# Graph-attention layers on Trainium2: target scores as three bfloat16 numbers, spread by a bfloat16 zero-one matrix

## The chip, the core and the metric

The kernel runs on one core of a Trainium2 chip. The core has five instruction streams: TensorE (PE in the profile, its weight loads PEld), VectorE (DVE), ScalarE (ACT), GpSimd (POOL) and SyncE (SP, which here only starts transfers). The metric is the device time of one run in microseconds. Three runs of the kernel before gave a median of 2871.9 us (2867.6 to 2875.4).

## The reference

The input is `x` of 8 batches x 2048 nodes x 128 features and one symmetric adjacency matrix with about 17 neighbours per node. Four layers follow one another: attention, graph, attention, graph. The change touches the two graph layers only, numbered 1 and 3. Such a layer computes

```python
h = x @ W
s_i = h @ a_src
s_j = h @ a_dst
e = s_i[:, :, None] + s_j[:, None, :]
e = jnp.where(e >= 0, e, NEG_SLOPE * e)
e = jnp.where(adj[None, :, :] == 0, -jnp.inf, e)
att = jax.nn.softmax(e, axis=-1)
out = jnp.einsum('bij,bjd->bid', att, h)
y = out + x
```

and then a layer norm. `s_i` is the score of the target node, the one that receives; `s_j` that of the source, its neighbour.

## The kernel before

**Sparse tiling.** The 2048 nodes are cut into 32 units of 64 target nodes. The neighbours of a unit's targets are listed in up to 9 tiles of 128 slots, one slot being one edge; they are handled as `TG = 5` steps `t`, four of two tiles each and a last one of a single tile. On the 128 partitions of a gathered tile lie 128 edges. The four batches of each half of the batch (`HB = 4`, two halves) lie beside each other, so a slot has 2 x 4 scores.

**Rows.** Each layer leaves a table in DRAM with one row per node: for a graph layer the source score, the 128 features and a one per batch. An indirect transfer that GpSimd starts (`gather`, L1711) fetches the 128 rows of a tile. Its buffers are six `kv` rings, and each ring is shared by four tiles in a graph layer.

**Targets.** A target's score is made a layer earlier, when that layer's result is projected (`project`): `spread_out` (L1613) writes it into the constant tile `self.t[:, u]`, 128 partitions x 16 columns. The partitions are the targets of the two halves in groups of 32, the 16 columns are 4 groups x 4 batches, and all but the own group is zero.

**The zero-one matrices.** Tile `hot` (float32, 960 columns) has two parts. Columns 0 to 639 say for each target which slots are its own (`fetch`): ScalarE writes the distance of the slot number from the middle of a target's slots (L1439), VectorE compares it with half the length (L1446). Columns 640 to 959 say for each slot which target it has (`slots`, L1357, called at L1464). For the first four units (`LATE = 4`) a second piece is added (L1457 to L1461).

**A unit of a graph layer.** `opened_graph` spreads the target scores over the slots: one matmul per step `t` with 128 columns of `hot` as the stationary operand and `self.t` as the moving one, into the PSUM tile `ps_te` (L2091). VectorE takes a large number from the scores of empty slots and writes `te` (`mask`, L2106 to L2115). Then, for each step, in `graph`: VectorE adds target and source score and applies the slope (`score`, L2030 and L2037), ScalarE takes the exponential (L2042), VectorE multiplies the exponentials by the zero-one matrix, giving `w` (`fold`, L2052), and PE multiplies `w` with the gathered rows and adds up in PSUM (`add`, L2068: 16 matmuls for a step of two tiles, 8 for the last). After five steps `after_graph` divides, adds the residual, norms, and projects to the next layer's table (layer 1) or writes the output (layer 3).

**The order of the work.** No loop order is written down for the engines. Each operation is given to a planner (`Plan`) with its estimated cost per engine, a key (layer x 1000 + unit x 5 + step, less or plus an offset) and the tiles it reads and writes. The planner plays the run through with these costs and takes on each engine the ready operation of lowest key; an operation is only taken when its buffers are free. The order that comes out is fixed into the program, each engine then runs its list strictly in order, and waits are semaphores. So a changed cost or a new operation can shift the order of everything that the planner decides later. Operations marked `port=True` are kept by the planner from running on VectorE and GpSimd at once; a gather (`port="wait"`) isn't started while one runs. Work with a lowered key is prepared ahead: the score matmuls have key base - 3, the building of `hot` base - 8, gathers key - 12.

Of the kernel before, what the change touches and what calls it, by code (L numbers as in the profile page):

```python
# [11 lines left out]
BF16 = mybir.dt.bfloat16  # L12
F16 = mybir.dt.float16
F8 = mybir.dt.float8e5
I32 = mybir.dt.int32
AF = mybir.ActivationFunctionType
ALU = mybir.AluOpType
# [3 lines left out]
P = 128  # L21
# [11 lines left out]
GROUP = 32  # L33
UNIT = 2 * GROUP
TG = 5
TILES = 2 * TG - 1
GS = TG * P
# [3 lines left out]
HOT = GS + 2 * TG * GROUP  # L41
# [8 lines left out]

SBUF_BUFS = {
    "kv": 6, "hot": 3, "hot8": 5, "x": 4, "q_sb": 2, "rows": 3, "at": 1, "r": 2, "x1": 2, "hidden": 1, "normed": 2,
    "xnew": 2, "trows": 2, "s": 2, "ex": 7, "var": 2, "rstd": 2, "rc": 2, "te": 2, "e": 4, "w": 3,
    "cand": 2, "aux": 3, "aux16": 3, "unit_aux": 2, "some": 2, "rank_e": 2, "pick": 1,
    "gap": 1, "late": 1,
}
# [544 lines left out]
class Plan:  # L601
# [35 lines left out]
    def cell(self, tag, shape, dtype=F32, name=None):  # L637
        pool = self.pools[tag]
        return Cell(tag, lambda: pool.tile(shape, dtype, name=name or tag, tag=tag))

    def op(self, costs, fn, key, reads=(), writes=(), joins=(), holds=(), shares=(), port=False, dma=0):


        o = Op({e: us * self.share for e, us in costs.items()}, fn, key, port, dma)
        shares = [*shares, *(c.whole for c in (*reads, *writes, *joins, *holds) if c.whole)]
        before = set()
        for c in reads:
            before.update(c.writers)
        for c in writes:
            before.update(c.writers)  # L650
            before.update(c.readers)
        for c in joins:
            before.update(c.readers)
        for c in reads:
            c.readers.append(o)
        for c in writes:
            c.writers, c.readers = [o], []
        for c in joins:
            c.writers.append(o)
        before.update(w for c in holds for w in [c.owner, *c.writers] if w)  # L660
        for c in dict.fromkeys([*writes, *joins, *reads, *holds, *shares]):
            if c.tag:
                if not c.owner:
                    c.owner = o
                    o.allocs.append(c)
                c.left += 1
                o.cells.append(c)
        for b in before:
            b.next.append(o)
        o.waits = len(before)  # L670
        o.behind = [c.owner for c in (*shares, *joins) if c.tag and c.owner is not o]
        self.ops.append(o)
# [130 lines left out]
class Sparse:  # L803
# [602 lines left out]
    def fetch(self, n, u, key):  # L1406

        x = self.cell("x", [P, CH])
        self.op(
            {"SP": 0.45},  # L1410
            lambda e: e.dma_start(out=x.tile, in_=self.xd[u] if n else self.xt_in[u]),
            key,
            reads=[self.x_at[u] if n else self.gates[20]],
            writes=[x],
            dma=P * CH * 4,
        )
        hot = self.cell("hot", [P, HOT])
        if n == 0 and u < KEPT:
            hot8 = self.kept[u]
            self.op({"ACT": 1.05}, lambda e: e.copy(hot.tile, hot8.tile), key - 15, reads=[hot8], writes=[hot])  # L1420
            return x, hot
        if LAYERS[n] is MHA:
            hot8 = self.cell("hot8", [P, HOT], F8)
            self.op(
                {"SP": 0.45},
                lambda e: e.dma_start(out=hot8.tile, in_=self.hots[u]),
                key,
                reads=[self.hots_at[u]],
                writes=[hot8],
                holds=[hot],  # L1430
                dma=P * HOT,
            )
            self.op({"ACT": 1.05}, lambda e: e.copy(hot.tile, hot8.tile), key + 4, reads=[hot8], writes=[hot])
            return x, hot

        ends, oht = self.ends[:, u, :], lambda: hot.tile[:, 0:GS]
        self.op(
            {"ACT": 0.82},
            lambda e: e.activation(oht(), self.slot, AF.Abs, bias=ends[:, 0:1]),  # L1439
            key + 4,  # L1440
            reads=[self.ends_at[u]],
            writes=[hot],
        )
        self.op(
            {"DVE": 0.4},
            lambda e: e.tensor_scalar(oht(), oht(), ends[:, 1:2], None, ALU.is_le),  # L1446
            key + 4,
            writes=[hot],
            port=True,
        )  # L1450
        if u < LATE:
            after = self.cell("late", [P, P])
            self.op(
                {"ACT": 0.3}, lambda e: self.late_targets(e, after.tile, u), key + 4, reads=[self.ends_at[u]], writes=[after], holds=[hot]
            )

            def both(e):  # L1457
                shared = hot.tile[:, GS - P : GS]
                e.scalar_tensor_tensor(shared, after.tile, self.late_ends[:, u, 1:2], shared, ALU.is_le, ALU.add)

            self.op({"DVE": 0.25}, both, key + 4, reads=[after], writes=[hot])  # L1461
        self.op(
            {"DVE": 0.5},
            lambda e: self.slots(e, hot.tile, self.owner[:, u]),  # L1464
            key + 4,
            reads=[self.idx_at[u]],
            writes=[hot],
            port=True,
        )
        return x, hot  # L1470

    def whole(self):

# [517 lines left out]
    def graph(self, n):  # L1991
        hb = self.HB
        width = hb * (P + 2)
        op, cell = self.op, self.cell
        made = {}
        for u, i in self.sequence(LATE):
            base = n * STRIDE + u * TG
            if not i:
                made[u] = self.opened_graph(n, u, base)
            x, hot, te, outs, banks = made[u]  # L2000
# [5 lines left out]
            if u < LATE:  # L2006
                t, at = i, u * 2 * PAIRS + 2 * i if i < PAIRS else LATE * 2 * PAIRS + u
                key = base + i if i < PAIRS else n * STRIDE + LATE * TG - 2 + u / LATE
            else:
                t = i if u % 2 == 0 else (i - 1) % TG  # L2010
# [35 lines left out]
            w = cell("w", [P, 2 * hb, 2, GROUP])  # L2046

            def fold(e, t=t, hot=hot, e8=e8, w=w, tiles=tiles):
                oh = hot.tile[:, GS + 2 * t * GROUP : GS + (2 * t + 2) * GROUP].rearrange("p (j c) -> p j c", j=2)
                for j in range(0, 2, tiles):  # L2050
                    shape = [P, tiles, 2 * hb, GROUP]
                    e.tensor_tensor(  # L2052
                        w.tile[:, :, j : j + tiles, :].rearrange("p x j c -> p j x c"),
                        oh[:, j : j + tiles].unsqueeze(2).to_broadcast(shape),
                        e8.tile[:, 0:tiles].unsqueeze(3).to_broadcast(shape),
                        ALU.mult,
                    )
# [23 lines left out]
    def opened_graph(self, n, u, base):  # L2081
        hb = self.HB
        op, cell = self.op, self.cell
        x, hot = self.fetch(n, u, base - 12)

        ps = cell("m", [P, TG, 4 * hb], name="ps_te")
        te = cell("te", [P, TG, 2, 2, hb])

        def spread(e, u=u, ps=ps, hot=hot):
            for t in range(TG):  # L2090
                e.matmul(  # L2091
                    ps.tile[:, t, :],
                    lhsT=hot.tile[:, t * P : (t + 1) * P],
                    rhs=self.t[:, u, :],
                    start=True,
                    stop=True,
                )

        op({"PE": 0.8}, spread, base - 3, reads=[hot, self.t_at[u]], writes=[ps], holds=[te])

        def mask(e, u=u, ps=ps, te=te):
            last = TG - 1
            scores = ps.tile.rearrange("p t (h j b) -> p t h j b", h=2, j=2)
            empty = self.empty[:, u, 0 : 2 * last].rearrange("p (t j) -> p t j", j=2).unsqueeze(3)
            for hf in range(2):
                e.tensor_tensor(  # L2106
                    te.tile[:, 0:last, hf],
                    scores[:, 0:last, hf],
                    empty.to_broadcast([P, last, 2, hb]),
                    ALU.subtract,  # L2110
                )

            own = te.tile[:, last, :, 0, :]
            e.tensor_scalar(own, scores[:, last, :, 0, :], self.empty[:, u, 2 * last :], None, ALU.subtract)
            e.tensor_tensor(own, scores[:, last, :, 1, :], own, ALU.add)  # L2115

        op({"DVE": 0.6}, mask, base - 3, reads=[ps, self.idx_at[u]], writes=[te])

        if u % 2 == 0:
            outs = [cell("q", [P, 4, CH], name="acc_q")]  # L2120
            banks = [lambda outs=outs, k=k: outs[0].tile[:, k, :] for k in range(2)]
        else:
            outs = [cell("acc", [P, CH]), cell("m", [P, CH], name="acc_m")]
            banks = [lambda outs=outs, k=k: outs[k].tile for k in range(2)]
        return x, hot, te, outs, banks
# [165 lines left out]
```

## Time and profile before

| what | before |
|---|---|
| median of 3 runs | 2871.9 us |
| profiled execution, whole | 3119.97 us |
| its span, first to last instruction | 3118.2 us |
| mean granted TensorE clock | 0.883 |
| PE busy / instructions | 2427.8 us (78%) / 21668 |
| DVE busy / instructions | 2312.8 us (74%) / 3782 |
| ACT busy | 1432.0 us (46%) |
| POOL busy | 2126.9 us (68%) |
| bytes moved by DMA | 1022.48 MB, mean 328 GB/s |
| matmuls of the target scores | first 1137.8 us, last 3074.0 us |

The profile is one execution with the hardware profiler on, and it is 248 us longer than the median run; durations of single instructions come from it. Each row of its groups names a line and engine, the operation, the tiles written and read with their shapes, a count, the busy time and the mean of one in ns, and after the last bar how long the engine had been idle just before such instructions and what ended that. A float32 matmul leaves two matmul records and two weight-load records, a 16-bit one leaves one of each. "issue" is time in which an engine waited for nothing that the profile shows. "remote" or "an unknown queue" is a releaser that the trace can't name. The chain of waits goes back from the last instruction to what released it, step by step, so it shows what the end hung on.

The layers follow one another with some overlap; the two graph layers are seen at the score matmuls, from about 1140 to 1620 us and from about 2620 to 3100 us.

### The profile page before, as it was taken

To read this page: it belongs to the slowest core of one execution; us is meant where nothing else is said; L and a number is where in the kernel's file an instruction comes from. 1 tells how busy PE (TensorE), PEld (TensorE's weight loads), DVE (VectorE), ACT (ScalarE), POOL (GpSimd) and SP (SyncE) were. 2 spreads that over 40 slices of the span, in tenths; PEclk is the share of its full clock that TensorE was granted. 3 is DMA by queue.
4 is the path that set the end of the run, shared out by engine and by line. 5 is a ranking of instruction groups with operands and counts; after the bars stand their busy time and mean duration, and the time that the engine had idled before them with its cause. 6 is when DMAs were issued, how large, how long until landed. Compare 5 with 4: busy or idle time off the path is not lost.

```text
span 3118.2 us, 59203 instructions
## 1 busy us (share of the span) xinstructions
PE 2427.8 (78%) x21668; PEld 1343.1 (43%) x21668; DVE 2312.8 (74%) x3782; ACT 1432.0 (46%) x4900; POOL 2126.9 (68%) x1465
## 2 busy tenths in 40 slices
PE   6677877878888858877886888888888876777775
PEld 4423333333333346655664333333333335555554
DVE  8798988998999944444436889989899984555555
ACT  6455455555554425444443444445454432333332
POOL 1387877888888645555543888888888864655552
PEclk8788888899999978998877999999999987877787
DMA  7888889898899879999996899999999977999994
GB/s 301 331 328 304 315 312 345 325 355 334 345 382 357 314 255 332 353 353 338 334 320 244 344 363 376 367 379 375 369 358 373 379 264 242 341 314 315 315 312 157
DMA packets 248057, 1022.48 MB, mean 328 GB/s; under 512 B 39184, under 2 KB 52880, under 8 KB 175856
## 3 DMA queue, kind: packets, MB, share of 16 engines
q0 software_dynamic: 166464, 864.44, 74.0%
q1 hardware_dynamic: 81296, 154.18, 13.6%
q8 instruction: 174, 2.85, 0.4%
q14 instruction: 123, 1.01, 0.1%
HBM read 978.23 MB, written 88.08 MB: 342 GB/s over the span
## 4 chain that ended last, share of the span: by engine, by line
PE 33%; DVE 19%; issue 17%; POOL 12%; DMA 12%; ACT 4%; another core or an unknown queue 2%; POOLq 0%; SPq 0%; DVEq 0%; ACTq 0%
DMA kv<-table,idx 8%; POOL kv L1817 7%; DVE kv L1784 7%; POOL kv L1711 5%; PE acc_q L2068 5%; PE qe L1772 4%; PE acc L1869 4%; DVE s L1791 3%; PE ps_c L1535 3%; PE acc_m L2068 2%; PE ps_p L1573 2%; PE acc L2068 2%; PE ps_f L1545 2%; DMA hot<-hots 2%
## 5 line engine op out<-in xcount | busy, mean ns | idle before, releaser
L1711 POOL DMA_INDIRECT kv<-table,idx x1152 | 1189.4, 1032 | 756.9 <-issue 281.3
L1817 POOL TENSOR_TENSOR kv<-kv,ex 128x2048 f32<-128x2048 f32 x260 | 923.4, 3567 | 94.9 <-ACT ex L1801 90.6
L1784 DVE TENSOR_TENSOR kv<-qe,kv 128x2048 f32<-128x2048 f32 (+1 forms) x320 | 661.8, 2068 | 94.3 <-DMA kv<-table,idx 44.7
L1791 DVE TENSOR_REDUCE s<-kv 128x128 f32<-128x2048 f32 (+1 forms) x320 | 660.5, 2064 | 12.5
L1772 PE MATMUL qe<-q_sb,hot 32*128 32x512 f32 (+1 forms) x2304 | 393.4, 685 | 144.3 <-DVE kv L1784 134.6
L1869 PE MATMUL acc<-kv,hot 128*32 128x512 f32 (+1 forms) x2304 | 362.9, 640 | 54.1 <-POOL kv L1817 43.9
L2052 DVE TENSOR_TENSOR w<-hot,e 128x512 f32<-128x512 f32 (+1 forms) x384 | 222.4, 598 | 200.4 <-remote 64.6
L2068 PE MATMUL acc_q<-kv,w 128*32 128x129 f32 (+1 forms) x4608 | 255.5, 318 | 100.9 <-issue 69.0
L2068 PEld LDWEIGHTS acc_q<-kv,w 128*32 128x32 f32 (+1 forms) x4608 | 178.8, 130 | 168.7 <-issue 117.4
L1772 PEld LDWEIGHTS qe<-q_sb,hot 32*128 32x128 f32 (+1 forms) x2304 | 106.5, 194 | 333.6 <-DVE kv L1784 223.7
L1801 ACT ACTIVATE ex<-s 128x128 f32<-128x128 f32 (+1 forms) x320 | 95.3, 298 | 286.9 <-DVE s L1791 245.5
L1647 ACT ACTIVATE junk<-ps_c 128x128 f32<-128x128 f32 x492 | 136.0, 276 | 161.1 <-PE ps_c L1535 131.3
L2068 PE MATMUL acc<-kv,w 128*32 128x129 f32 (+1 forms) x2304 | 146.2, 321 | 67.6 <-issue 29.3
L2068 PE MATMUL acc_m<-kv,w 128*32 128x129 f32 (+1 forms) x2304 | 163.3, 315 | 42.7 <-issue 42.0
L1545 PE MATMUL ps_f<-x,W 128*128 128x512 f32 (+1 forms) x264 | 164.1, 715 | 39.8 <-ACT x L1690 18.3
L1511 ACT COPY trows<-ps_p 128x258 f32<-128x258 f32 (+1 forms) x237 | 112.4, 476 | 161.0 <-PE ps_p L1575 77.8
L1535 PEld LDWEIGHTS ps_c<-centre,r 128*128 128x128 f32 x1024 | 131.4, 200 | 107.4 <-DVE r L1941 56.7
L1535 PE MATMUL ps_c<-centre,r 128*128 128x128 f32 x1024 | 154.4, 296 | 26.0 <-DVE r L1941 21.0
L1961 ACT ACTIVATE hidden<-ps_f,b 128x512 f32<-128x512 f32 (+1 forms) x130 | 87.8, 676 | 154.9 <-PE ps_f L1545 136.8
L1680 ACT ACTIVATE normed<-ps_c,rstd 128x128 f32<-128x128 f32 x494 | 143.7, 368 | 9.6 <-issue 3.5
L1869 PEld LDWEIGHTS acc<-kv,hot 128*32 128x32 f32 (+1 forms) x2304 | 55.1, 114 | 213.7 <-issue 108.9
L1522 PE MATMUL ps_t<-ident,normed 128*128 128x128 f32 x638 | 119.8, 309 | 32.3 <-ACT xnew L1690 18.1
(204 smaller groups left out, 3761.0 us busy)
## 6 DMA issues: line engine op xcount, KB each, us to landing
x<-xd SPq DMA_DIRECT2D x96, 256.0 KB
xd<-xnew SPq DMA_DIRECT2D x93, 256.0 KB
kv<-table,idx POOLq DMA_INDIRECT x1152
table<-trows SPq DMA_DIRECT2D x128, 130.0 KB
kv<-adj_dram SPq DMA_DIRECT2D x16, 1024.0 KB
table<-trows SPq DMA_DIRECT2D x32, 512.0 KB
table<-trows SPq DMA_DIRECT2D x64, 256.0 KB
kv<-xk_dram SPq DMA_DIRECT2D x8, 1024.0 KB
```

Of the source, the lines that this page charges most:

```text
L1535: e.matmul(ps.tile[:, cols], lhsT=flat(x.tile)[:, cols], rhs=self.centre, start=True, stop=True)
L1545: lambda e: e.matmul(ps.tile, lhsT=w, rhs=x.tile, start=True, stop=True),
L1647: e.activation(self.junk, x, AF.Square, scale=P**-0.5, accum_out=var.tile[:, b, 1:2])
L1680: e.activation(out, in_, AF.Copy, scale=by)
L1711: e.indirect_dma_start(out=rows(kv.tile, j), out_offset=None, in_=self.tables[n][0:nodes], in_offset=bass.IndirectOffsetOnAxis(ap=self.idx ...
L1772: e.matmul(qe.tile[:, j, hf, :], lhsT=hot.tile[rows, t * P : (t + 1) * P], rhs=q.tile[rows, :], start=True, stop=True,)
L1784: e.tensor_tensor(k, qe.tile[:, 0:tiles].rearrange("p j h c -> p (j h) c"), k, ALU.mult)
L1791: e.tensor_reduce(s.tile[:, 0 : tiles * heads].rearrange("p (q c) -> p q c", q=2 * tiles), k, axis=mybir.AxisListType.X, op=ALU.add,)
L1817: e.tensor_tensor(v, v, w.unsqueeze(3).to_broadcast([P, 2 * tiles, heads // 2, HD]), ALU.mult)
L1869: e.matmul(out[rows, :], lhsT=hot.tile[:, col : col + GROUP * (3 - tiles)], rhs=rhs[:, 2 * j + hf, :], start=(t == 0), stop=(t == TG - 1),)
L2052: e.tensor_tensor(w.tile[:, :, j : j + tiles, :].rearrange("p x j c -> p j x c"), oh[:, j : j + tiles].unsqueeze(2).to_broadcast(shape), e ...
L2068: e.matmul(acc(b)[at : at + GROUP * (3 - tiles), :], lhsT=w.tile[:, hf * hb + b, j : j + 3 - tiles, :].rearrange("p j c -> p (j c)"), rhs= ...
```

## The change

The matrix `hot` of a graph layer is held as bfloat16 in the first half of the same tile, and the distances before the compare as float16 in the same place. The target scores of a unit are split on VectorE into three bfloat16 numbers each: the score rounded, the rest rounded, and the rest of that; the rests overwrite `self.t`. The three go side by side into one matmul per step with 48 columns in place of 16, all operands bfloat16, and VectorE adds the three in a reduction out of PSUM before it masks. The new tile `thirds` has two buffers. The weight product reads its zeros and ones from the bfloat16 matrix. The planner's cost of the score matmuls goes from 0.8 to 0.6, of the masking from 0.6 to 0.85, and the split is entered with 0.4. The attention layers are not edited.

```diff
-    "xnew": 2, "trows": 2, "s": 2, "ex": 7, "var": 2, "rstd": 2, "rc": 2, "te": 2, "e": 4, "w": 3,
+    "xnew": 2, "trows": 2, "s": 2, "ex": 7, "var": 2, "rstd": 2, "rc": 2, "te": 2, "thirds": 2, "e": 4, "w": 3,
...
-        ends, oht = self.ends[:, u, :], lambda: hot.tile[:, 0:GS]
+        ends = self.ends[:, u, :]
+
+        def numbers():
+            return hot.tile[:, 0 : HOT // 2].bitcast(F16)[:, 0:GS]
+
+        def low():
+            return self.low(hot)
+
...
-            lambda e: e.activation(oht(), self.slot, AF.Abs, bias=ends[:, 0:1]),
+            lambda e: e.activation(numbers(), self.slot, AF.Abs, bias=ends[:, 0:1]),
...
-            lambda e: e.tensor_scalar(oht(), oht(), ends[:, 1:2], None, ALU.is_le),
+            lambda e: e.tensor_scalar(low()[:, 0:GS], numbers(), ends[:, 1:2], None, ALU.is_le),
...
-                shared = hot.tile[:, GS - P : GS]
+                shared = low()[:, GS - P : GS]
...
-            lambda e: self.slots(e, hot.tile, self.owner[:, u]),
+            lambda e: self.slots(e, low(), self.owner[:, u]),
...
+    def low(self, hot):
+
+        return hot.tile[:, 0 : HOT // 2].bitcast(BF16)
...
-                oh = hot.tile[:, GS + 2 * t * GROUP : GS + (2 * t + 2) * GROUP].rearrange("p (j c) -> p j c", j=2)
+                oh = self.low(hot)[:, GS + 2 * t * GROUP : GS + (2 * t + 2) * GROUP].rearrange("p (j c) -> p j c", j=2)
...
-        ps = cell("m", [P, TG, 4 * hb], name="ps_te")
+        thirds = cell("thirds", [P, 3, 4 * hb], BF16)
+
+        def split(e, u=u, thirds=thirds):
+            rest = self.t[:, u, :]
+            for k in range(3):
+                e.tensor_copy(thirds.tile[:, k, :], rest)
+                if k < 2:
+                    e.tensor_tensor(rest, rest, thirds.tile[:, k, :], ALU.subtract)
+
+        op({"DVE": 0.4}, split, base - 5, writes=[self.t_at[u], thirds])
+        ps = cell("m", [P, TG, 3, 4 * hb], name="ps_te")
...
-                    ps.tile[:, t, :],
-                    lhsT=hot.tile[:, t * P : (t + 1) * P],
-                    rhs=self.t[:, u, :],
+                    ps.tile[:, t].rearrange("p k c -> p (k c)"),
+                    lhsT=self.low(hot)[:, t * P : (t + 1) * P],
+                    rhs=thirds.tile.rearrange("p k c -> p (k c)"),
...
-        op({"PE": 0.8}, spread, base - 3, reads=[hot, self.t_at[u]], writes=[ps], holds=[te])
+        op({"PE": 0.6}, spread, base - 3, reads=[hot, thirds], writes=[ps], holds=[te])
...
-            scores = ps.tile.rearrange("p t (h j b) -> p t h j b", h=2, j=2)
+            e.tensor_reduce(
+                te.tile.rearrange("p t h j b -> p t (h j b)"),
+                ps.tile.rearrange("p t k c -> p t c k"),
+                axis=mybir.AxisListType.X,
+                op=ALU.add,
+            )
+            scores = te.tile
...
-        op({"DVE": 0.6}, mask, base - 3, reads=[ps, self.idx_at[u]], writes=[te])
+        op({"DVE": 0.85}, mask, base - 3, reads=[ps, self.idx_at[u]], writes=[te])
```

More of the change, by code (lines that the diff above doesn't have):

```diff
@@ L2084, in opened_graph, with spread @@
         x, hot = self.fetch(n, u, base - 12)
-        ps = cell("m", [P, TG, 4 * hb], name="ps_te")
+        thirds = cell("thirds", [P, 3, 4 * hb], BF16)
[7 more added lines that the diff above has]
+        ps = cell("m", [P, TG, 3, 4 * hb], name="ps_te")
         te = cell("te", [P, TG, 2, 2, hb])
-        def spread(e, u=u, ps=ps, hot=hot):
+        def spread(e, thirds=thirds, ps=ps, hot=hot):
             for t in range(TG):
                 e.matmul(
-                    ps.tile[:, t, :],
-                    lhsT=hot.tile[:, t * P : (t + 1) * P],
-                    rhs=self.t[:, u, :],
+                    ps.tile[:, t].rearrange("p k c -> p (k c)"),
+                    lhsT=self.low(hot)[:, t * P : (t + 1) * P],
+                    rhs=thirds.tile.rearrange("p k c -> p (k c)"),
                     start=True,
```

## The prediction

> **What bounds the kernel now.** I read the page's engine rows first, then its DMA queues, then the two stretches in which the graph layers run (layer 1 at 1140 to 1620 us, layer 3 at 2620 to 3100 us; both are found from the first and last start of the scores' matmuls), and last the chain of waits inside them. The table by stretch gives these two rows; the columns are length, busy time of PE, PE weight load, DVE, ACT and POOL with counts, the granted PE clock, the DMA engines' share and GB/s.
>
> ```profile
> 1140.00:1620.00 480.00, 383.16 (x5052) 286.39 (x5053) 213.62 (x768) 218.19 (x779) 270.60 (x259) 0.87 0.93 331
> 2620.00:3100.00 480.00, 347.61 (x4898) 267.56 (x4898) 261.26 (x869) 182.42 (x738) 266.33 (x252) 0.78 0.87 300
> ```
>
> A graph layer has 32 units, so one unit takes 15.0 us. PE is busy for 12.0 us of it in layer 1 and 10.9 us in layer 3, DVE for 6.7 and 8.2 us. DMA is near its end: 0.93 and 0.87 of its 16 engines over the stretches. The page's queue rows say the same of the whole run:
>
> ```profile
> q0 software_dynamic: 166464, 864.44, 74.0%
> q1 hardware_dynamic: 81296, 154.18, 13.6%
> ```
>
> With the two instruction queues this is 88.1% of 3118.2 us, or 2747 us of DMA busy time. The timed runs take 2871.9 us, only 125 us more. If packets take as long there, little that an engine saves can come through. This is the reason for halving a gain below.
>
> The chain of waits, its pieces added up by me over these stretches, holds in layer 1: PE 225 us, "issue" 137, POOL 50, DMA 25, DVE 22, ACT 19; in layer 3: PE 228, "issue" 87, DVE 72, unknown queues 42, ACT 27, DMA 14, POOL 14. So PE is what ends last, with its own gaps: the answer on waits in layer 3 names what PE and the gathers stand for.
>
> ```profile
> PE acc_q L2068 <- issue: 33.8, 63, 4.9
> PE acc L2068 <- DVE w L2052: 17.1, 13, 2.8
> ...
> DVE te L2106 <- PE ps_te L2091: 34.9, 9, 6.0
> ...
> POOL kv L1711 <- PE acc_m L2068: 60.8, 26, 5.9
> ```
>
> Read: gathers wait for PE to give back a ring, DVE waits for PE's score matmuls and not the reverse, and PE waits for DVE less than for its own issue. PE's work on the scores has 20.7 us of the chain in layer 1 and 30.4 us in layer 3.
>
> **The change, part by part.** Each number is per unit; there are 64 units in the two layers.
>
> *The score matmuls.* These rows, for the whole run, give the old form and the nearest 16-bit form:
>
> ```profile
> L2091 PE MATMUL ps_te<-t,hot 128*128 128x16 f32 x640 | 97.2, 285 | 8.9 <-issue 7.2 <-ACT trows L1511 0.9 <-DVE r L2158 0.3
> L1288 PE MATMUL ps_l<-unit_aux,hot 128*128 128x86 f16 x160 | 12.6, 213 | 16.0 <-ACT hot L1268 11.9 <-DVE hot L1280 3.2 <-ACT trows L1511 0.7
> ```
>
> The 320 float32 matmuls have 640 records (two each) and 97.2 us, 1.52 us per unit. The 16-bit form has one record per matmul and 12.6/160 = 0.079 us each; five are 0.39 us. The new ones have 48 columns against 86, so this is no underestimate by width; 0.3 to 0.5 us are its ends. Saved: 1.52 - 0.39 = 1.13 us, 72 us in all, of which the chain held 51.1 of 97.2 us. On the path: 51.1 x 1.13/1.52 = **-38 us**. PE also loses 10 of about 316 instructions per unit (5052 x 2 / 32), half of them weight loads; of the 224 us of "issue" on the chain that share is 7 us at most. I take **-4**, with 0 and -7 as ends, since the page doesn't say that each instruction carries an equal gap.
>
> *The split, new on DVE.* Three copies and two subtractions of 128x16. The near rows are the score additions and the leaky slope, both of that size:
>
> ```profile
> L2030 DVE TENSOR_TENSOR e<-te,kv 128x16 f32<-128x16 f32 x256 | 46.2, 180 | 0.6 <-issue 0.3
> L2037 DVE SCALAR_TENSOR_TENSOR e<-e 128x16 f32<-128x16 f32 x256 | 45.2, 177 | 8.8
> ```
>
> 2 x 0.18 + 3 x 0.165 (copies of 4 elements took 0.160) = 0.86 us. It depends on the table's projection of the layer before, so it is ready long ahead, and on one of two buffers that the score matmuls of two units earlier give back. The masking of that earlier unit waits for the same matmuls, and its key is lower, so it stands in front of the split and takes the wait that DVE already has (the 34.9 us above). I count no new wait. The split's cover is DVE's idle time, 6.8 us per unit in layer 3 and 8.3 in layer 1. What lies behind it on DVE are the weight products that PE waits for. DVE holds 94 us of the chain against 475 us of busy time in the stretches, 20%; so of 64 x 0.86 = 55 us I take **+11**. Ends: 0 (all in idle time) and +55 (no cover).
>
> *The adding of three.* One reduction of 240 elements out of PSUM, in front of the masking. Reductions of 320 and of 80 elements took 478 and 225 ns:
>
> ```profile
> L1325 DVE TENSOR_REDUCE rank_e<-pick 128x8 f32<-128x320 f32 x32 | 15.3, 478 | 0.0
> ```
>
> By the line between them, 225 + 160 x 1.05 = 0.39 us; no row here has so small a reduction from PSUM, but the product that reads PSUM at 2048 elements (2281 ns) and the one that doesn't (2277) are equal, so I take 0.40. The masking then reads SBUF and not PSUM: no saving counted. It stands between PE's scores and the first weights of a unit, and the masking has 8.2 us of the chain for 43 us busy, 19%. 64 x 0.40 x 0.19 = **+5**; ends 0 and +26.
>
> *The target matrix in 16 bits.* ScalarE writes 640 numbers: 0.823 us in float32, 0.833 us in float16 in the setup, so nothing. The slot compare with a float16 output took 479 ns against 482: nothing. The weight product reads its zeros and ones in 16 bits and the rest in float32; no row mixes inputs at that place. I keep its 686 ns; ends -0.1 and +0.1 us per tile. The one that may gain is the compare of 640:
>
> ```profile
> L1446 DVE TENSOR_SCALAR hot<-hot,ends 128x640 f32<-128x640 f32 x64 | 35.6, 556 | 10.5 <-ACT hot L1439 8.0 <-issue 2.3
> ```
>
> Here a rule is weighed. The Trainium skill, "VectorE: DVE Perf Modes", section on the perf-mode tier table, says that a one-source operation goes at two elements per cycle in float32 and four in 16 bits, from SBUF. The trace has no wide 16-bit one: 128 elements took 248 ns in float16 and 230 ns in float32, which shows no gain at that width. By the rule, the 128-to-640 slope of the float32 rows (0.64 ns per element) halves and the compare falls to about 0.40 us; by the row it stays 0.55. I take the rule, since the row is too narrow to show a slope. That is 10 us of DVE, of which the chain held 4.7 of 35.6 us: **-1**.
>
> The second rule speaks against the change. "SBUF — State Buffer", section "Who interferes with whom", says that a copy or cast from SBUF to SBUF that runs in a two-port mode takes the port pair that GpSimd needs to write gather descriptors, and that the later one waits in full. The three copies qualify, and the plan isn't told (the split has no port mark). The row: gathers took 985 ns at least, 993 in the median and 1510 at most in layer 3, with half-microsecond compares of that kind already beside them. By the rule the copies could block 3 x 0.165 = 0.5 us per unit, 32 us of POOL; by the row the common gather sees nothing. POOL holds 64 us of the chain's 979, 7%, so even the rule makes +2. I take **+1**.
>
> *What is not changed.* No transfer, table, gather or matmul on gathered rows. The planner's costs do change (DVE +0.65, PE -0.2 us per unit), so its greedy order shifts from the first split on. I can't work that out from a trace; I give it plus or minus 9 us, 0.3%, around every case.
>
> **The sum** against the profiled execution (span 3118.2 us, with what lies around it 3120.0): -38 - 4 + 11 + 5 - 1 + 1 = -26 us. What is late next is the gathers' traffic. Layer 1 runs its middle, 1200 to 1500 us, at a DMA share of 0.95 to 0.98, where hardly anything can come off; layer 3 has 0.92 in its middle. The timed run is 247 us shorter than the profiled one with the same bytes, so it is closer to that end still. I let 60% through: -16 us. From the median of 2871.9 us, **2856 us**; own range 2838 to 2863.
>
> **The rivals.**
> *No change.* DMA is the end in both layers when nobody profiles. For it: 2747 us of busy time in 2872. Against it: the gathers stood idle for 61 + 39 us behind PE's last matmuls in 410 us of layer 3. Time: 2872, give or take 9.
> *Slower: DVE's order becomes the bound.* The added 0.86 + 0.40 - 0.15 = 1.1 us per unit, 71 us in all, falls between masking and the weight product, and PE waits for it. For it: PE already waits for weights (17.1 us in one row above), and in layer 3 DVE is busy 54%. Against: DVE has 6.8 us idle per unit. It decides once more than a third of the added DVE time lies on the path while DMA swallows PE's saving: 71/3 = +24, so 2894 us.
> *It doesn't do what it says:* that the 16-bit matmuls still go as two records each. Then PE saves less than 0.8 us and the first rival's time holds; the one-record float16 row speaks against it.
>
> **How the numbers follow.** Forecast 0.56, no change 0.20, slower 0.24 (the failed-split case lies in no change). The range takes the forecast's low end (2838, and to 2834 for all of the sum with a good order) and most of the slower rival, to 2890. A measurement of this kernel can tell about 0.3%, 9 us, from no change; so faster means below 2863, slower above 2881. Part of the forecast's own spread crosses into "same", and part of "same" out of it.
>
> **What would show it.** Score records from 640 to 320 with weight loads near 100 ns and about 25 us busy; split operations near 0.17 us each; a reduction near 0.40 us; the compare at 0.40 us; PE's share of the chain in both layers down by about 38 us; DMA share up by one or two hundredths. I am wrong if DVE's wait for ACT or the PE's wait for weights grows by more than the scores shrink, or if the graph stretches don't shorten at all while PE is freed.

## The result, and the profile after

The changed kernel is slower: median 2893.8 us of 6 runs against 2872.5 of 6, ratio 1.0067 with a 95% interval of 1.0047 to 1.0087. The prediction was 2856 us and faster.

What the engines do went as worked out. These are the rows of the changed kernel's groups for the edited operations (operation and tiles, busy time and mean ns after the first bar):

```profile
L2112 PE MATMUL ps_te<-thirds,hot 128*128 128x48 bf16 x320 | 19.3, 188 | 2.5 <-DVE hot L1453 1.4 <-DVE r L2185 0.8 <-ACT trows L1522 0.2
```

```profile
L2102 DVE CAST thirds<-t 128x16 bf16<-128x16 f32 x192 | 53.5, 279 | 4.4
...
L2124 DVE TENSOR_REDUCE te<-ps_te 128x80 f32<-128x240 f32 x64 | 25.7, 401 | 6.2 <-PE ps_te L2112 5.8 <-PE acc_q L2079 0.2
...
L1453 DVE TENSOR_SCALAR hot<-hot,ends 128x640 bf16<-128x640 f16 x64 | 24.8, 388 | 3.6 <-ACT hot L1446 3.2
...
L2104 DVE TENSOR_TENSOR t<-t,thirds 128x16 f32<-128x16 f32 x128 | 22.6, 177 | 4.4
```

The score matmuls have 320 records and 19.3 us where they had 640 and 97.2; the reduction takes 401 ns (0.40 was worked out), the compare 388 (0.40), a subtraction 177. One row is off: the casts' mean is 279 ns, against 165 worked out. Their median is 175, so some must be very long; that comes up again below.

The span of this profile is 2902.4 us, *shorter* than the 3118.2 us of the profile that the prediction was read from, although the kernel is slower. So the first question is about that profile.

### The profile page after: what moved, and what is told of

Its sections match the earlier page's. It is cut to its first block, busy times and chain, and to the rows that moved or that the text cites. A ratio compares the mean times of both kernels' runs of the same rounds, so it can differ in the third digit from the quotient of the medians.

```text
span 2902.4 us, 58939 instructions
## 1 busy us (share of the span) xinstructions
PE 2203.9 (76%) x21348; PEld 1208.3 (42%) x21348; DVE 2397.0 (83%) x4168; ACT 1429.1 (49%) x4897; POOL 2126.7 (73%) x1466
## 2 busy tenths in 40 slices
DMA packets 248059, 1022.48 MB, mean 352 GB/s; under 512 B 39184, under 2 KB 52880, under 8 KB 175856
## 4 chain that ended last, share of the span: by engine, by line
DMA 29%; DVE 24%; PE 19%; issue 12%; POOL 11%; ACT 4%; SPq 0%; POOLq 0%; DVEq 0%; ACTq 0%
DMA kv<-table,idx 24%; DVE kv L1795 8%; POOL kv L1828 6%; POOL kv L1722 5%; PE qe L1783 4%; DVE s L1802 4%; DMA hot<-hots 4%; PE acc L1880 4%; PE ps_c L1546 2%; DVE w L2063 2%; PE ps_f L1556 2%; PE ps_y L1982 1%; DMA table<-trows 1%; PE ps_p L1584 1%; DVE kv L1828 1%
## 5 line engine op out<-in xcount | busy, mean ns | idle before, releaser
L2079 PE MATMUL acc_q<-kv,w 128*32 128x129 f32 (+1 forms) x4608 | 201.0, 312 | 134.0 <-DVE w L2063 117.1
L2063 DVE TENSOR_TENSOR w<-hot,e 128x512 f32<-128x512 bf16 (+1 forms) x384 | 221.0, 598 | 42.3 <-ACT e L2053 32.4
L2079 PEld LDWEIGHTS acc_q<-kv,w 128*32 128x32 f32 (+1 forms) x4608 | 161.0, 128 | 165.1 <-DVE w L2063 133.5
L2041 DVE TENSOR_TENSOR e<-te,kv 128x16 f32<-128x16 f32 (+1 forms) x320 | 58.1, 182 | 167.2 <-DMA kv<-table,idx 161.3
L2079 PE MATMUL acc<-kv,w 128*32 128x129 f32 (+1 forms) x2304 | 120.4, 310 | 87.2 <-DVE w L2063 72.8
L1556 PE MATMUL ps_f<-x,W 128*128 128x512 f32 (+1 forms) x264 | 152.5, 669 | 39.1 <-ACT x L1701 27.0
L2053 ACT ACTIVATE e<-e 128x16 f32<-128x16 f32 (+1 forms) x320 | 65.9, 213 | 187.4 <-DVE e L2048 175.8
```

The costliest lines, as they stand in the source:

```text
L1556: lambda e: e.matmul(ps.tile, lhsT=w, rhs=x.tile, start=True, stop=True),
L2063: e.tensor_tensor(w.tile[:, :, j : j + tiles, :].rearrange("p x j c -> p j x c"), oh[:, j : j + tiles].unsqueeze(2).to_broadcast(shape), e ...
L2079: e.matmul(acc(b)[at : at + GROUP * (3 - tiles), :], lhsT=w.tile[:, hf * hb + b, j : j + 3 - tiles, :].rearrange("p j c -> p (j c)"), rhs= ...
```

## The experiments

Ratios are to the kernel before, run on the same chip between the same runs; the 95% interval stands in brackets.

**A second profile of the kernel before.** No edit.

> The kernel before, unchanged, for a second profile. The first one has a span of 3118 us where timed runs take 2872; the changed kernel's profile has 2902 where its runs take 2894. If the first profile was disturbed, this one has a span near 2875 us, graph layers of about 400 us each instead of 480, PE issue gaps well below 12% of the chain, and a DMA share near 0.97 in the graph layers. Then the chain that the prediction read (PE on top) was that of one disturbed execution. If profiling this kernel always costs that much, the span is near 3118 us again.

Measured: 2879.1 us, span 2877.4 us. The page's first line and its row of the DMA engines' rate in 40 slices:

```profile
span 2877.4 us, 59203 instructions
...
GB/s 281 314 339 333 325 293 359 311 327 351 308 366 379 353 362 297 371 407 405 408 404 379 278 371 381 382 386 380 372 370 373 378 370 257 367 403 409 404 403 257
```

In the slices of the graph layers (18 to 21, 36 to 39) the transfers go at 403 to 409 GB/s; the first profile had 331 and 300 in the prediction's two rows. The first execution was out of the ordinary: the spans of all other profiles here lie between 2867 and 2930 us. In layer 3 PE's products into `acc_q` waited 33.8 us for "issue" there and 11.7 us here. What disturbed it isn't known. The middle of the two graph layers, by the table of stretches (columns as in the prediction), first in this second profile of before, then in the changed kernel:

```profile
1130.00:1530.00 400.00, 323.35 (x5096) 260.27 (x5096) 213.76 (x759) 222.32 (x784) 264.87 (x258) 0.89 1.01 400
2460.00:2840.00 380.00, 272.93 (x4939) 233.16 (x4939) 254.88 (x845) 180.43 (x723) 282.56 (x267) 0.83 1.01 398
```

```profile
1140.00:1540.00 400.00, 294.13 (x4860) 230.31 (x4853) 240.72 (x923) 220.93 (x776) 263.13 (x256) 0.88 1.01 396
2480.00:2860.00 380.00, 248.29 (x4754) 208.49 (x4754) 282.97 (x1024) 178.61 (x716) 278.64 (x265) 0.79 1.01 394
```

The share of the DMA engines, last but one, is 1.01 in all four. I read this as stages that hang on bytes, with PE's 29 and 25 us less, and DVE's 27 and 28 us more, under that; no run here changes the bytes. The waits say it too; in layer 3 of the second profile of before VectorE waits for gathered rows, PE for VectorE, and the gathers hardly for PE:

```profile
DVE e L2030 <- DMA kv<-table,idx: 77.1, 57, 20.8
...
PE acc_q L2068 <- DVE w L2052: 56.0, 25, 19.3
...
POOL kv L1711 <- PE acc_m L2068: 2.6, 4, 1.2
```

That last wait had 60.8 us in the first profile. The chain of waits in layer 3 turns round with it; first the first profile (2640 to 3050 us), then the second (2460 to 2840 us):

```profile
by line: issue 18.8%; PE acc_q L2068 14.9%; PE acc_m L2068 10.9%; another core or an unknown queue 8.2%; PE acc L2068 8.2%; PE ps_te L2091 6.5%; PE ps_c L1535 6.3%; DVE w L2052 5.6%; DMA kv<-table,idx 3.4%; POOL kv L1711 3.4%; ACT junk L164
```

```profile
by line: DMA kv<-table,idx 43.0%; issue 17.7%; POOL kv L1711 11.1%; DVE w L2052 4.9%; PE acc_q L2068 3.9%; ACT junk L1647 2.0%; PE ps_c L1535 1.9%; DVE normed L2172 1.8%; ACT normed L1680 1.8%; PE ps_te L2091 1.8%; PE acc L2068 1.7%; DVE r 
```

The score matmuls, `ps_te`, hold 1.8% of the second chain, about 7 us, where the prediction counted 30.4. (In the second profile the chain can't be followed back as far as layer 1.)

So where were the 21 us lost? I counted the gathers in both timelines (288 per layer) and took the start of the 96th and of the last one of each layer, changed kernel less second profile of before:

```
gather number          96    288    576    864   1152
second profile, us  456.4 1079.3 1546.1 2414.3 2844.6
changed kernel, us  +14.4   +8.9  +11.0  +14.3  +22.9
```

It is 14 us behind by the 96th gather, in layer 0, an attention layer that the change doesn't edit. What is new there are the splits of the first two units of the next graph layer, and the order of the work. Each column is of single executions, and the second profile of before is up to 12 us from another kernel in the same order (the new instructions in the old order, below), so the table is a hint of the place and no more.

**Theories.** *Port:* these early casts wait for GpSimd. *VectorE's work* in the graph layers (the prediction's slower rival). *Order:* the planner's new order is a worse one. The timeline of the changed kernel at one early split of layer 2 (start, length, engine, line, operation):

```profile
1697.59 7.33 POOL L1828 TENSOR_TENSOR kv<-kv,ex 128x2048 f32<-128x2048 f32 x2
1698.90 6.06 DVE L2102 CAST thirds<-t 128x16 bf16<-128x16 f32 x1
...
1705.00 0.18 DVE L2104 TENSOR_TENSOR t<-t,thirds 128x16 f32<-128x16 f32 x1
```

A cast of 16 numbers per partition takes 6.06 us and ends 0.04 us after GpSimd's two multiplies (1697.59 + 7.33 = 1704.92 us). The first casts of the four early splits, two in each attention layer, took 4.72, 1.23, 3.40 and 6.06 us, and each ended with a multiply. That is 14.7 us more than 0.175 us each, on an engine that is busy for about 90% of those layers. All 192 casts together wait about 20 us; most of the rest are 33 casts beside the start of a gather, held by up to 0.3 us each, like this one:

```profile
230.99 1.03 POOL L1722 DMA_INDIRECT kv<-table,idx  x1 [0.16 <-POOL kv L1828]
...
231.54 0.46 DVE L2102 CAST thirds<-t 128x16 bf16<-128x16 f32 x1
```

The profile that the prediction was read from has such a wait already, in the second piece of the matrix (L1459), an operation of 0.34 us in the median that isn't marked as a port user either:

```profile
1059.69 7.32 POOL L1817 TENSOR_TENSOR kv<-kv,ex 128x2048 f32<-128x2048 f32 x2
1060.50 6.67 DVE L1459 SCALAR_TENSOR_TENSOR hot<-late,late_ends,hot 128x128 f32<-128x128 f32 x1
```

**Mark the split as a port user.**

```diff
-        op({"DVE": 0.4}, split, base - 5, writes=[self.t_at[u], thirds])
+        op({"DVE": 0.4}, split, base - 5, writes=[self.t_at[u], thirds], port=True)
```

> The changed kernel with the split marked as a user of the shared port, so that the planner keeps it off GpSimd's multiplies. Port theory (casts of the first two units of each graph layer wait inside the attention layer before for GpSimd, 12 casts with about 20 us of waiting, VectorE being the busiest engine there): casts at most 0.5 us, and 10 to 20 us faster than the changed kernel, ratio to before 1.000 to 1.003. Theory of VectorE's work in the graph layers: no more than 3 us faster, ratio 1.006. Theory of the order alone: anything within 0.5%, with no link to the casts.

Measured: 1.0077 (1.0056 to 1.0098). A miss for the port theory as I had put it, but the row of the casts says that the edit didn't do what it should:

```profile
L2102 DVE CAST thirds<-t x192: 160/174/6269, 701.5 to 2824.6; 128x16 bf16<-128x16 f32 x192
```

The longest is still 6.27 us (minimum, median and maximum stand after the count). The planner keeps the two apart in its own simulated time, and the chip's time differs from that. This cast started beside a gather, 0.65 us ahead of two multiplies, and ended with the second one. The casts still wait 9 us at multiplies in all, so the test told little about the port and gave one more order.

**Leave the split out.** The matmuls read a constant tile in place of `thirds`, and the split operation is gone.

> The changed kernel without the split: the matmuls read a constant bfloat16 tile, so the scores of the targets are left out of the result. It has all the rest: 16-bit matrix, one-record matmuls, the reduction. Port theory: ratio to before 0.995 to 1.001, as the loss came with the casts alone. Theory of VectorE's work in the graph layers: the reduction remains (0.4 us per unit) but not the 0.86 us of the split; two thirds of the loss goes, ratio 1.002. Order theory: no forecast, within 0.5% of before.

Measured: 1.0056 (1.0036 to 1.0076). Without any cast most of the loss is still there, but the order changed with it as well, so by itself this doesn't separate them.

**The planner's costs alone**, in the kernel before:

```diff
-        op({"PE": 0.8}, spread, base - 3, reads=[hot, self.t_at[u]], writes=[ps], holds=[te])
+        op({"PE": 0.6}, spread, base - 3, reads=[hot, self.t_at[u]], writes=[ps], holds=[te])
...
-        op({"DVE": 0.6}, mask, base - 3, reads=[ps, self.idx_at[u]], writes=[te])
+        op({"DVE": 0.85}, mask, base - 3, reads=[ps, self.idx_at[u]], writes=[te])
```

> The kernel before with the planner's costs of the score matmuls and of the masking as in the changed kernel (0.6 and 0.85), nothing else: the same instructions in another order from layer 1 on. Order theory: slower by 5 to 20 us, ratio 1.002 to 1.007. Port theory and theory of VectorE's work: ratio 0.998 to 1.002. It also gives the size of what a shift of the order does by itself.

Measured: 1.0039 (1.0017 to 1.0061). The same instructions in another order are slower. The planner has the same operations and costs here as in the kernel without the split, so these two are a pair in one order: the new instructions but the split have 1.0056, the old ones 1.0039. The intervals overlap, and by the two means most of what was left without the split is the order. From here on instructions and order had to be crossed.

**New instructions in the old order.** The planner sees the operations and costs of before; the split rides in the slot compare, and its three numbers go to the unused half of the matrix's tile.

```diff
-            lambda e: self.slots(e, low(), self.owner[:, u]),
+            lambda e: (self.slots(e, low(), self.owner[:, u]), self.split(e, hot, u)),
...
-        op({"PE": 0.6}, spread, base - 3, reads=[hot, thirds], writes=[ps], holds=[te])
+        op({"PE": 0.8}, spread, base - 3, reads=[hot, self.t_at[u]], writes=[ps], holds=[te])
```

> All new instructions of the change (16-bit matrix, split, one-record matmuls, reduction) in exactly the order of the kernel before: the planner is given the old operations and costs, and the split is issued inside the slot compare of the unit, with the three numbers kept in the unused half of the matrix's tile. Order theory: ratio to before 0.996 to 1.002. Theory of VectorE's work in the graph layers: 1.005 to 1.008, as in the changed kernel. Port theory: 0.997 to 1.001, since no cast runs deep in an attention layer.

Measured: 1.0012 (0.9995 to 1.0030), so neither a cost nor a gain of the instructions can be seen. From the last gather of the layer before to its own last one, layer 1 takes 469 us against 467 in the second profile of before, and layer 3 takes 431 against 430, although PE is busy 63 us less in the run.

**Old instructions in the new order.** An empty operation with the split's cost and buffers, and the changed costs:

```diff
+        thirds = Cell("thirds", lambda: None)
+        op({"DVE": 0.4}, lambda e: None, base - 5, writes=[self.t_at[u], thirds])
...
-        op({"PE": 0.8}, spread, base - 3, reads=[hot, self.t_at[u]], writes=[ps], holds=[te])
+        op({"PE": 0.6}, spread, base - 3, reads=[hot, thirds], writes=[ps], holds=[te])
```

> The counterpart: the old float32 instructions in exactly the order of the changed kernel (the planner is given the changed costs and an empty operation in place of the split). Order theory: ratio to before 1.005 to 1.008, as in the changed kernel. Theory of VectorE's work and port theory: 0.998 to 1.002, since neither casts nor a reduction are there.

Measured: 1.0033 (1.0016 to 1.0050): about half of the changed kernel's loss comes with the order alone, less than the order theory gave.

Together with the changed kernel, and with the next one below, these make a table (ratio, 95% interval):

```
                                   old order                new order
old instructions                   1 (the kernel before)    1.0033 (1.0016 to 1.0050)
new, split in the slot compare     1.0012 (0.9995 to 1.003) 1.0022 (1.0006 to 1.0038)
new, early split (as changed)      -                        1.0067 (1.0047 to 1.0087)
```

**The changed kernel with late splits.** The new order exactly, its split operation empty, and the split in the slot compare:

```diff
+        thirds = Cell("thirds", lambda: None)
+        op({"DVE": 0.4}, lambda e: None, base - 5, writes=[self.t_at[u], thirds])
...
-            lambda e: self.slots(e, low(), self.owner[:, u]),
+            lambda e: (self.slots(e, low(), self.owner[:, u]), self.split(e, hot, u)),
```

> The changed kernel in exactly its own order, but with the splits issued inside the slot compare of their unit; the planner's split operation is empty. No cast runs in the middle of an attention layer any more, and all the other new work stays. If the early casts, which wait for GpSimd, are what the new instructions cost on top of the new order (0.34%): ratio to before 1.002 to 1.005, like the old instructions in the new order. If it is the new work in the graph layers: 1.005 to 1.008, as in the changed kernel.

Measured: 1.0022, in the table. The order of ScalarE, GpSimd and the transfers is the same as in the changed kernel, that of VectorE too but for the splits, and 0.45% is gone, 13 us (5 to 20 by the two intervals). Its casts:

```profile
L1487 DVE CAST hot<-t x192: 159/174/422, 1085.1 to 2812.8; 128x16 bf16<-128x16 f32 x192
```

None is longer than 0.42 us, and none starts before 1085 us. The 13 us have the size of the 14.7 us of waiting seen in the trace: the early casts are what the new instructions cost on top of the order. The late splits also no longer wait for a buffer of `thirds`, but VectorE stood idle for only 4.4 us before the casts of the changed kernel, and 4.4 before the subtractions.

The time between gathers shows it in place. From the 24th to the 48th gather, in layer 0, where the casts of 4.72 and 1.23 us lie, the changed kernel takes 97.1 us; in its own order with late splits it is 90.7, and with the old instructions 88.8. In all profiles here, the three with a long cast there have 97 to 99 us and the eleven without have 89 to 93. By layers, from the last gather of the one before (in layer 0 from the first gather), one execution each:

```
us to the layer's last gather          layer 0  layer 1  layer 2  layer 3
before, second profile                   956.0    466.8    868.2    430.3
new instructions in the old order        947.8    469.1    862.9    431.3
old instructions in the new order        953.7    467.1    863.2    444.5
new, late splits, new order              936.7    467.2    864.7    442.1
changed kernel                           966.7    468.9    871.6    438.9
```

Single executions scatter by 10 us and more in layer 0, so only the direction counts: in one order the new instructions don't shorten the graph layers, the new order is 8 to 14 us longer in layer 3, and the changed kernel is longest in layers 0 and 2, the two with early casts.

**Further draws of the order.** One planner constant, the time of a signal between engines, is moved by one thousandth of a microsecond, here up; two of the runs below have 0.139.

```diff
-    HOP = 0.14
+    HOP = 0.141
```

> The kernel before with one planner constant, the time of a signal between engines, at 0.141 in place of 0.140 us: the same instructions, another order everywhere. If the order of the kernel before is a better one than its neighbours: ratio 1.003 to 1.008. If orders scatter about the same mean: anything within 0.997 to 1.003. Port theory and theory of VectorE's work: within 0.998 to 1.002.

Measured: 1.0074 (1.0047 to 1.0102).

> A further draw of the order for the old instructions, planner constant at 0.139. If the order of the kernel before is a good draw: ratio above 1.002. If orders scatter evenly about it: as likely below 1 as above.

Measured: 1.0043 (1.0028 to 1.0057). With the three above, the old instructions have now been in four other orders: 1.0033, 1.0039, 1.0043, 1.0074, none as good as the first.

> The changed kernel with the same planner constant at 0.141: another draw of the order for the new instructions. If the order of the kernel before is a good draw and all others are alike: ratio to before 1.003 to 1.008 and equal to that of the kernel before at 0.141 within 0.3%. If the new instructions cost by themselves: above that of the kernel before at 0.141 by 0.5% or more.

Measured: 1.0171 (1.0132 to 1.0211), beyond what I gave. By the gather count it is 28 us behind the second profile of before in layer 2 and 13 in layer 0. Its casts hold 43.7 us in all against some 34 without waiting; of these 10 us, 5 are waits at multiplies. The rest of the loss goes with the order, as far as these runs tell.

> A further draw for the changed kernel, planner constant at 0.139. Order theory: 1.003 to 1.017, the scatter of the other draws. If the changed kernel is above the kernel before in every draw by 0.5% or more, its early casts or its planner's cost of the split have a part in it.

Measured: 1.0066 (1.0041 to 1.0091). The kernel before at the same constant has 1.0043; the difference is 0.23%, 6.6 us, and its casts wait 6.3 us at multiplies. The two orders aren't the same, and the intervals overlap, so this fits and shows nothing by itself.

> A second pair for the new instructions alone: they run, with the split inside the slot compare, in exactly the order of the kernel before at 0.141, which had 1.0074. If the new instructions cost and save nothing in a given order: 1.0055 to 1.010. If they cost by themselves: above 1.011.

Measured: 1.0107 (1.0076 to 1.0138) against 1.0074 for the old instructions in that order. The intervals overlap; the three pairs of new against old in one order are +0.12%, -0.11% and +0.33%, and the pair without the split is +0.17%. An effect of the new instructions by themselves isn't shown, and one of 0.1 or 0.2% isn't excluded.

## Why the prediction was wrong, step by step

**PE's saving: the size was right, its place in the chain wasn't.** 1.13 us per unit were worked out; 97.2 - 19.3 = 78 us against the first profile, 86.0 - 19.3 = 67 against the second, are 1.0 to 1.2. Put on the path as -38 us, they gave nothing that shows: with the new instructions in the old order PE is busy 63 us less than in the second profile (2188.6 against 2251.9 us) and the ratio is 1.0012. This is the step that failed first. That run holds PE's saving and VectorE's new work together, so the one could hide the other; but without the split, in one order, the ratio is no better (1.0056 against 1.0039). The chain with PE on top was that of one execution, 248 us longer than the runs; in the second profile the score matmuls hold about 7 us of layer 3's chain. I had noticed the length and the 2747 us of DMA time, and used them to halve the gain where they meant to cancel it. The first rival, "no change", had the mechanism of the graph layers, and the evidence against it, gathers that wait 61 + 39 us for PE, was the first profile's alone (2.6 + 0.6 us in the second). The sign of being wrong that the prediction named, graph stretches that don't shorten while PE is freed, is what came.

**"It is ready long ahead": the split's early place.** I used this to count no new wait for the split. It is true, and it is why the planner puts the first two splits of each graph layer into the attention layer before, next to GpSimd's multiplies. The rule of the Trainium skill that I weighed ("SBUF — State Buffer", "Who interferes with whom": whoever starts first has the port pair for its whole instruction) was set against gathers in the graph layers alone, at +1 us. Its price was against the multiplies: 14.7 us of waiting in the trace, 13 us by the run with late splits. The row of L1459 in the profile of before, 6.67 us for an operation of 0.34, had shown that price before the change. Beside gathers the wait went the other way round than I had put it: gathers keep their median of 0.99 us, and the casts are held, by about 5 us in the changed kernel. Of the split's own cost in the graph layers, +11, nothing shows.

**"Plus or minus 9 us" for the order.** It was too small, and the sign was not free. Four other orders of the old instructions cost 9.5 to 21 us, none saved anything; the changed kernel's own order costs 0.33%, about 9.5 us, with the old instructions, and 0.10%, 3 us, with the new ones. That the order of the kernel before is an unusually good one fits this; why it is better isn't shown.

**The sum as it came out:** PE and VectorE in the graph layers about 0 (between -3 and +9 by the pairs), order +3 to +10, early casts +10 to +13, together about the +19 that the ratio gives. The slower rival gave 2894 us (its own sum, 2871.9 + 24, is 2896), and 2893.8 was measured, but this is luck: its mechanism was VectorE between masking and weights in the graph layers, and there the new instructions in the old order have no cost that shows.

**Right:** one record per matmul, the sizes of reduction and compare (the rule of the Trainium skill, "VectorE: DVE Perf Modes", the perf-mode tier table, four elements per cycle in 16 bits, gave 0.40 us, measured 0.388), of casts that aren't held (175 ns in the median, 165 worked out), of the weight product (598 ns in the mean of both its shapes before and after), and that no transfer changes (1022.48 MB in both).

No version here beats the kernel before. The new instructions in the old order equal it.

## What to carry to other kernels

When a profile is 8% longer than the timed runs, take a second one before reading a chain in it, and test the chain against the stage's bytes: where the transfers were full here, 63 us less of PE gave nothing that shows. Where a planner or scheduler sets the order, any edit is also a new draw of the order; hold the order fixed (give the planner the old operations, or an empty one) before putting a change of half a per cent down to instructions. A new operation that is "ready early" will be run early: look at what is beside it there, not where it is used, and look through the profile for small operations with a few very long records: they mark the place where the wait already happens.

## What was not expected of the hardware

A cast of 128x16 float32 numbers that started while GpSimd multiplied ended 0.03 to 0.04 us after a multiply, in all four cases of the changed kernel; twice it sat out two multiplies in a row (4.72 and 6.06 us against 0.175), where the rule named above speaks of one instruction. One of 6.27 us started beside a gather and was held through the two multiplies behind it. The instructions behind such a cast on VectorE wait too. Marking the two as exclusive in a simulated plan didn't keep them apart on the chip. And the same instructions took 0.4 and 0.7% longer in the orders that came of a planner constant moved by one nanosecond.
